# Splitting late weight loads and bias foldings, and reordering two steps beside causal attention, in a fused cross-attention and transformer block

## The chip, the cores and the metric

The kernel runs on one core of one Trainium2 chip. The metric is the device time of one execution in microseconds (us); lower is better. The kernel before took 955.61 us, the median of three runs that lay between 954.59 and 956.64.

## The reference

Two layers are computed for 16 batches of 256 tokens with 256 features; both use 16 heads of width 16, everything in float32.

```python
# layer 0: cross attention with RMS norms and a mask over the context (all true here)
Q = rmsnorm(x, g_q) @ Wq;  K, V = rmsnorm(ctx, g_c) @ (Wk, Wv)
x = rmsnorm(x + softmax(Q K^T * hd**-0.5, masked) V @ Wo, g_out)
# layer 1: a block with causal self attention, cross attention, and an MLP of 1024
h = ln(x);  q, k = rope(h @ sa_wq + b), rope(h @ sa_wk + b);  v = h @ sa_wv + b
x = x + causal_attention(q, k, v) @ sa_wo + sa_bo
h = ln(x);  q = rope(h @ ca_wq + b);  k, v = rope(y @ ca_wk + b), y @ ca_wv + b
x = x + attention(q, k, v) @ ca_wo + ca_bo
x = x + gelu(ln(x) @ fc1_w + fc1_b) @ fc2_w + fc2_b
```

The gains and biases of the layer norms are not applied to the activations. The kernel folds them into the weights ("gain": each row of the weight is multiplied) and into the biases ("bias": the norm's bias times the weight is added to the projection's bias).

## The kernel before, in words

There are 48 attentions: three for each batch, of type 0 (cross attention of the first layer), 1 (causal self attention) and 2 (cross attention of the second layer). `ORDER` (line 31) is a string of 48 digits that says which type comes at each place `i`; the batch is the count of that digit so far. The whole order is written out by hand in one schedule (line 878 on): a loop over `i`, and in it a loop over the blocks `n` of scores of attention `i`, four for types 0 and 2 and three for the causal type 1. Each engine executes its instructions in the order in which the schedule issues them. After the 48 attentions comes an MLP over pairs of batches, which takes the last quarter of the time.

At block `n` the schedule issues, always in this order: the scores of block `n` (`scores`, line 475: matmuls of line 488 into two PSUM tiles `S`, then two exponentials of ScalarE at line 499, then for causal blocks the masking selects of GpSimd at line 506), the product of probabilities and values of block `n-1` (`value`, line 517: matmuls of line 527 into the single PSUM tile `A`), and then the pieces of neighbouring attentions:

- `n = 0`: `end` of attention `i-1` (VectorE copies `A` to SBUF, line 544; SP sends it to DRAM and fetches the sums of the softmax and the outputs back turned, lines 552 and 557), `divide` of `i-2` (line 578), statistics of the norms of `i+2`, and `q` of `i+1`.
- `n = 1`: `invert` of `i-1` (VectorE takes the reciprocal of the sums at line 564, for type 0 after a clamp at line 563; SP sends it to DRAM at line 566 and fetches it back broadcast at line 572), then `k` of `i+1`.
- the block before the last: `v` of `i+1` (line 468 or 460); the last block: the output projection of `i-2` (`project`, line 584 or 587) and the turn of the normed rows of `i+2` (`turn`, transposes at line 267).

For types 1 and 2, `q` and `k` go through `rotated` (line 390): ScalarE adds the bias out of PSUM (line 395), VectorE shuffles a copy (line 399) and multiplies by the cosine and sine tables (line 403). `q` then adds the two (line 419) and writes two masked copies, one for even and one for odd heads, into `qm` (lines 420 and 424, or 422); `k` adds into `kT` (line 447). For type 0, `k` is only a copy by ScalarE (line 449) and `q` two VectorE operations (line 414).

Which engine makes the second masked copy is decided by the attention that runs meanwhile:

```python
        att(i + 1).q(shared=a.causal)
...
            if shared:
                nc.scalar.activation(self.qm[:, :, 1, :], a, AF.Copy, scale=parity[1])
```

Only types 1 and 2 get this far in `q`. In `ORDER` a causal attention is followed by type 2 five times (i = 21, 28, 38, 40, 42) and by type 0 eleven times, so line 422 runs five times.

Batches are loaded when `att(i+3)` is of type 0: four DMAs of 256 KB (lines 94, 95, 99, 101) at the start of attention `i`. All of these, the hops through DRAM and the later weights are issued on SP's one queue, in order. The later weights are loaded at fixed places: `ca` (768 KB) at i = 3, `cao` (256 KB) and `fc1` (1 MB) at i = 4, `fc2` (1 MB) at i = 6, each at block n = 2 (lines 1000 to 1008).

The biases are folded by `fold_bias` (line 166): matmuls with the norm's bias as the stationary operand, a copy by ScalarE (line 180) and a hop to DRAM; `fold_back` (line 185) fetches the result back as columns, element by element, into `cols`. The cross attention and `fc1` share one folding (bias at i = 6, n = 3; back at i = 8, n = 2; the adds of `fold_ca_fc1` on VectorE, lines 201 to 203, at i = 8, n = 3, after the gain of `ca`, line 223). The gain of `fc1` is two GpSimd operations at i = 10 and 12, and `combine` (line 629) issues one GpSimd operation at a time at n = 1 of the non-causal attentions from i = 14 on.

Of the kernel before, what the change touches and what calls it, by code (L numbers as in the profile page):

```python
# [8 lines left out]
F32 = mybir.dt.float32  # L9
U8 = mybir.dt.uint8  # L10
I32 = mybir.dt.int32
AF = mybir.ActivationFunctionType
ALU = mybir.AluOpType
AX = mybir.AxisListType

P = 128
B, S, D = 16, 256, 256
H, HD = 16, 16
FF = 1024
NC = S // P  # L20
KC = D // P
# [7 lines left out]
N_ATT = 3 * B  # L29
# [16 lines left out]
def xattn_kernel(  # L46
# [21 lines left out]
    nc = tc.nc  # L68

    const = ctx.enter_context(tc.tile_pool(name="const", bufs=1))  # L70
    small = ctx.enter_context(tc.tile_pool(name="small", bufs=4))
    work = tc.alloc_tile_pool(name="work", bufs=2)

    def ctile(shape, name, dtype=F32):
        return const.tile(shape, dtype, tag=name, name=name)
# [31 lines left out]
    def load_w(t, aps, eng):  # L107
        at = 0
        for a in aps:
            m = a.shape[1]  # L110
            eng.dma_start(out=t[:, :, at : at + m], in_=a.rearrange("(k p) n -> p k n", p=P))
            at += m


    vec = ctile([P, NVEC + 2], "vec")
# [7 lines left out]
    sa_sb = ctile([P, KC, 3 * D], "sa")  # L123
    sao_sb = ctile([P, KC, D], "sao")
    ca_sb = ctile([P, KC, 3 * D], "ca")
    cao_sb = ctile([P, KC, D], "cao")
    fc1_sb = ctile([P, KC, FF], "fc1")
    fc2_sb = ctile([P, FF // P, D], "fc2")
# [7 lines left out]
    parity = [vec[:, NVEC + i : NVEC + i + 1] for i in range(2)]  # L136
# [6 lines left out]
    dram = ctx.enter_context(tc.tile_pool(name="dram", bufs=2, space=bass.MemoryType.DRAM))  # L143
# [19 lines left out]
    qk_bias = ctile([P, 4, KC], "qk_bias")  # L163
    fb1 = ctile([P, FF // P], "fb1")

    def fold_bias(sets):

        ps = dense_ps()
        w = len(sets) * D
        for n, items in enumerate(sets):  # L170
            for k in range(KC):
                for j, (t, at, vcol) in enumerate(items):
                    nc.tensor.matmul(
                        ps[32 * j : 32 * j + 32, n * D : (n + 1) * D],
                        lhsT=vec[:, vcol + k : vcol + k + 1].to_broadcast([P, 32]),
                        rhs=t[:, k, at : at + D],
                        start=(k == 0), stop=(k == KC - 1), skip_group_check=True,
                    )
        sb = work.tile([P, 2 * D], F32, tag="a", name="fold")
        nc.scalar.copy(sb[:, :w], ps[:, :w])  # L180
        hop = dram.tile([4, w], F32, tag=f"fold{len(sets)}", name="fold_hop", bufs=1)
        nc.sync.dma_start(out=hop, in_=sb[0:P:32, :w])
        return hop

    def fold_back(hop):

        w = hop.shape[1]
        cols = ctile([P, 4, w // D, KC], f"cols{w // D}")
        nc.sync.dma_start(
            out=cols.rearrange("p j n t -> p (j n t)"),  # L190
            in_=hop.rearrange("j (m p) -> p (j m)", p=P),
        )
        return cols
# [1 line left out]
    qk_cols = vec[:, V_QK : V_QK + 8].rearrange("p (n t) -> p n t", t=KC)  # L195

    def fold_sa(cols):
        nc.vector.tensor_tensor(qk_bias[:, 0:2], cols[:, 0:2, 0], qk_cols[:, 0:2], ALU.add)

    def fold_ca_fc1(cols):  # L200
        nc.vector.tensor_tensor(qk_bias[:, 2], cols[:, 0, 0], qk_cols[:, 2], ALU.add)
        nc.vector.tensor_copy(qk_bias[:, 3], qk_cols[:, 3])
        nc.vector.tensor_tensor(
            fb1.rearrange("p (j t) -> p j t", t=KC), cols[:, :, 1],
            vec[:, V_FC1B : V_FC1B + FF // P].rearrange("p (j t) -> p j t", t=KC), ALU.add,
        )

# [13 lines left out]
    def fold_gain(w, cols, vcol, chunks=range(KC), eng=nc.vector):  # L221
        for k in chunks:
            eng.tensor_scalar(
                w[:, k, cols], w[:, k, cols], vec[:, vcol + k : vcol + k + 1], None, ALU.mult
            )
# [82 lines left out]
    class Att:  # L308
# [96 lines left out]
                )  # L405
            return a, u

        def q(self, shared=False):
            ps = by_feature(self.hT, self.w, 0)
            self.qm = work.tile([P, KC, 2, S], F32, tag="qm", name="qm", bufs=2)  # L410
            if self.layer == 0:
                rq = self.rq.unsqueeze(1).to_broadcast([P, KC, S])
                for i in range(2):
                    nc.vector.scalar_tensor_tensor(
                        self.qm[:, :, i, :], ps, parity[i], rq, ALU.mult, ALU.mult
                    )
                return
            a, u = self.rotated(ps, 0)
            nc.vector.tensor_tensor(a, a, u, ALU.add)
            nc.vector.tensor_scalar(self.qm[:, :, 0, :], a, parity[0], None, ALU.mult)  # L420
            if shared:
                nc.scalar.activation(self.qm[:, :, 1, :], a, AF.Copy, scale=parity[1])
            else:
                nc.vector.tensor_scalar(self.qm[:, :, 1, :], a, parity[1], None, ALU.mult)

        def first_qk(self):

# [171 lines left out]
    def att(i):  # L599
        if 0 <= i < N_ATT:  # L600
            return atts.setdefault(i, Att(i))
        return None

    def do(i, *names):
        a = att(i)
        for name in names:
            if a is not None:
                getattr(a, name)()
# [269 lines left out]
    with tc.manual_schedule():  # L878
# [25 lines left out]
        for j in range(N_ATT):  # L904
            slot = next(i for i in range(max(j - 1, 0), N_ATT + 1) if (ORDER + [0])[i] != 1)
            kept.setdefault(slot, []).append(j)
        for i in range(N_ATT):
            a, last = att(i), att(i - 1)
            ahead = att(i + 3)
# [10 lines left out]
            for n in range(len(a.blocks)):  # L920
# [8 lines left out]
                if n == 0:  # L929
                    if i == 0:  # L930
                        a.v()
                        do(1, "spread")
                    late = finishing and i + 2 < N_ATT and att(i + 2).layer == 0
                    if not follows and not late and (finishing or not a.causal):
                        do(i + 2, "stats")
                    do(i - 1, "end")
                    if late:
                        do(i + 2, "stats")
                    do(i - 3, "finish")
                    if follows:  # L940
                        do(i + 2, "stats")
                    if not finishing:
                        do(i + 2, "norm")
                    if i == N_ATT - 3:
                        mlps[0].stats()
                    if i == N_ATT - 2:
                        mlps[0].norm()
                    do(i - 2, "divide")
                    if i == N_ATT - 1:
                        mlps[0].turn(nc.vector.tensor_copy)  # L950
                        mlps[0].keep()
                    if i + 1 < N_ATT:

                        att(i + 1).q(shared=a.causal)
                elif n == 1:
                    if last is not None:
                        last.invert(lambda: do(i + 2, "send"))
                    else:
                        do(i + 2, "send")
                    do(i + 2, "receive")  # L960
                    do(i + 1, "k")
                    if finishing:
                        do(i + 2, "norm")
                    for j in kept.get(i, ()):
                        att(j).keep()
                    if i == N_ATT - 1:
                        do(i - 2, "project")
                        mlps[1].norm()
# [23 lines left out]
                        out=rope_sb, in_=rope.rearrange("(c p) t d -> p c t d", p=P)  # L992
                    )
                if i == 1 and n == 3:
                    sa_hop = fold_bias([[(sa_sb, 0, V_B1), (sa_sb, D, V_B1)] * 2])
                if i == 2 and n == 2:
                    sa_cols = fold_back(sa_hop)
                if i == 2 and n == 3:
                    fold_gain(sa_sb, slice(0, 3 * D), V_G1)
                if i == 3 and n == 2:  # L1000
                    load_w(ca_sb, ca, nc.sync)
                if i == 3 and n == 3:
                    fold_sa(sa_cols)
                if i == 4 and n == 2:
                    load_w(cao_sb, [ca_o], nc.sync)
                    load_w(fc1_sb, [fc1], nc.sync)
                if i == 6 and n == 2:
                    load_w(fc2_sb, [fc2], nc.sync)
                if i == 6 and n == 3:
                    ca_hop = fold_bias(  # L1010
                        [[(ca_sb, 0, V_B2)] * 4, [(fc1_sb, j * D, V_B3) for j in range(4)]]
                    )
                if i == 8 and n == 2:
                    ca_cols = fold_back(ca_hop)
                if i == 8 and n == 3:
                    fold_gain(ca_sb, slice(0, D), V_G2)
                    fold_ca_fc1(ca_cols)
                if i in (10, 12) and n == 1:
                    fold_gain(fc1_sb, slice(0, FF), V_G3, [i // 12], nc.gpsimd)
                if n == 1 and i > 12 and not a.causal:  # L1020
                    next(combined, None)

        last = att(N_ATT - 1)
# [486 lines left out]
```

## Time and profile before

| quantity | value |
|---|---|
| median of three runs | 955.61 us (954.59 to 956.64) |
| the profiled execution, its own time | 953.12 us |
| its span from first to last instruction | 951.4 us |
| TensorE matmul (PE) busy | 936.0 us, 98% of the span |
| weight loads (PEld) busy | 551.9 us, 58% |
| VectorE (DVE) busy | 663.8 us, 70% |
| ScalarE (ACT) busy | 548.8 us, 58% |
| GpSimd (POOL) busy | 306.9 us, 32% |
| moved by DMA | 83.07 MB, mean 87 GB/s |
| exponentials of ACT, line 499 | 352 of 1022 or 1111 ns |
| granted TensorE clock | full throughout |

An attention is told apart in the trace by its first score matmul (line 488). From one such matmul to the next, an attention takes between 13.29 us (most causal ones) and 16.22 us (a non-causal one that turns rows and follows a causal one), so a few tenths of a microsecond of waiting show as a longer stretch of its kind. "Busy" of PE includes matmuls whose ends are modelled; the lengths of the stretches tell more than the share.

### The profile page before, as it was taken

The page shows a single profiled execution, that of the slowest core. Times are in us where ns is not written, and L with a number is a line of the kernel's source. Part 1 is how long each engine was busy: PE and PEld are TensorE (multiplying, and loading weights), DVE is VectorE, ACT ScalarE, POOL GpSimd, SP SyncE. Part 2 cuts the span into 40 slices and gives each one's busy share as a digit, 9 for nine tenths or more (in the row PEclk, how much of TensorE's full clock was granted, in tenths as well). Part 3 has the DMA queues.
Part 4 walks back from the last instruction along what each step waited for, and adds up shares of the span by engine and source line. Part 5 has one row for each costly group of instructions (what it writes and reads, how often), then busy time and mean ns, then how long its engine had stood idle before and what let it go on. Part 6 is the DMA issues. An engine that isn't in the chain of part 4 may idle for free.

```text
span 951.4 us, 29306 instructions
## 1 busy us (share of the span) xinstructions
PE 936.0 (98%) x12390; PEld 551.9 (58%) x12390; DVE 663.8 (70%) x1434; ACT 548.8 (58%) x777; POOL 306.9 (32%) x503
## 2 busy tenths in 40 slices
PE   8999999999999999999999999999999999999997
PEld 4444454445454455454454445455444799999997
DVE  4448666877777777867866767887877576676663
ACT  4666555766666665756656666666666634444440
POOL 3214353434344364243343423443233021222200
PEclk9999999999999999999999999999999999999999
DMA  9444353323232323222334222222222100000001
GB/s 302 135 118 155 123 170 82 119 77 116 86 121 71 113 83 127 64 88 92 100 124 127 80 82 68 72 70 71 71 69 72 57 23 20 13 14 24 23 24 47
DMA packets 99005, 83.07 MB, mean 87 GB/s; under 512 B 22570, under 2 KB 98350, under 8 KB 98866
## 3 DMA queue, kind: packets, MB, share of 16 engines
q1 hardware_dynamic: 98178, 80.58, 26.7%
q8 instruction: 99, 1.62, 0.7%
q10 hardware_dynamic: 688, 0.54, 0.2%
q14 instruction: 40, 0.33, 0.1%
HBM read 50.92 MB, written 30.17 MB: 85 GB/s over the span
## 4 chain that ended last, share of the span: by engine, by line
PE 88%; DVE 5%; DMA 3%; ACT 2%; issue 1%; SPq 1%; POOL 0%; ACTq 0%; DVEq 0%
PE S L488 18%; PE A L527 17%; PE d L287 15%; PE d L300 14%; PE upX L692 6%; PE A L790 5%; PE upZ L692 3%; PE downZ L790 3%; PE d L267 2%; PE d L790 2%; PE d L692 1%; ACT pt L499 1%; DVE u L399 1%; DVE u L403 1%; ACT a L395 1%; DVE a L403 1%
## 5 line engine op out<-in xcount | busy, mean ns | idle before, releaser
L499 ACT ACTIVATE pt<-S 128x1024 f32<-128x1024 f32 x224 | 217.2, 1022 | 111.4 <-PE S L488 111.4
L488 PE MATMUL S<-qm,kT 32*128 32x512 f32 (+1 forms) x1536 | 206.3, 600 | 2.9 <-DVE kT L447 2.9
L527 PE MATMUL A<-pt,va 128*32 128x256 f32 (+1 forms) x3072 | 188.7, 367 | 1.0 <-DVE av L544 1.0
L527 PEld LDWEIGHTS A<-pt,va 128*32 128x32 f32 x3072 | 80.1, 109 | 154.4 <-issue 104.1
L499 ACT ACTIVATE pt<-S,sy 128x1024 f32<-128x1024 f32 x128 | 135.6, 1111 | 46.5 <-PE S L488 45.9
L506 POOL TENSOR_SCALAR_AFFINE_SELECT pt<-pt 128x512 f32<-128x512 f32 x128 | 86.4, 693 | 70.0 <-ACT pt L499 69.7
L488 PEld LDWEIGHTS S<-qm,kT 32*128 32x128 f32 x1536 | 63.8, 183 | 71.5 <-issue 42.8
L231 POOL TENSOR_SCALAR r_ln<-bmv 128x2 f32<-128x2 f32 x48 | 14.1, 293 | 223.8 <-DVE bmv L250 222.7
L276 POOL TENSOR_TENSOR cur<-cur,bias 128x512 f32<-128x512 f32 x48 | 66.6, 1393 | 56.7 <-DVE xn L256 56.7
L395 ACT ACTIVATE a<-d,qk_bias 128x256 f32<-128x256 f32 x128 | 53.6, 471 | 47.8 <-PE d L287 37.5
L287 PE MATMUL d<-hT,sa 128*32 128x256 f32 x1024 | 61.1, 379 | 0.0
L587 DVE TENSOR_TENSOR cur<-d,cur 128x512 f32<-128x512 f32 x32 | 22.0, 688 | 50.3 <-PE d L300 50.2
L256 DVE TENSOR_SCALAR xn<-cur,bmv,r_ln 128x256 f32<-128x256 f32 x96 | 53.5, 606 | 0.8 <-POOL r_ln L232 0.3
L403 DVE TENSOR_TENSOR u<-u,turn 128x512 f32<-128x512 f32 x64 | 51.8, 810 | 0.0
L544 DVE COPY av<-A 128x512 f32<-128x512 f32 x47 | 32.4, 689 | 27.3 <-PE A L527 26.3
L403 DVE TENSOR_TENSOR a<-a,turn 128x512 f32<-128x512 f32 x64 | 47.8, 747 | 2.2
L399 DVE STREAM_SHUFFLE u<-a 128x512 f32<-128x512 f32 x64 | 47.6, 744 | 0.0
L730 ACT ACTIVATE g<-g,fb 128x256 f32<-128x256 f32 x96 | 41.0, 499 | 11.1 <-DVE g L719 11.1
L287 PEld LDWEIGHTS d<-hT,sa 128*32 128x32 f32 x1024 | 33.3, 110 | 22.0
L231 POOL TENSOR_SCALAR r_o<-ms_o 128x2 f32<-128x2 f32 x16 | 3.9, 243 | 123.0 <-DVE sq L239 113.4
L578 DVE TENSOR_TENSOR oT<-oT,inv 128x512 f32<-128x512 f32 x48 | 43.0, 896 | 0.5 <-DMA inv<-inv_hop 0.5
L785 DVE TENSOR_TENSOR g<-g,g 128x512 f32<-128x512 f32 x64 | 40.9, 681 | 0.0
(154 smaller groups left out, 1566.8 us busy)
## 6 DMA issues: line engine op xcount, KB each, us to landing
hop<-av SPq DMA_DIRECT2D x96, 256.0 KB
oT<-hop SPq DMA_DIRECT2D x96, 128.0 KB
inv<-inv_hop SPq DMA_DIRECT2D x96, 128.0 KB
xT<-in_xt SPq DMA_DIRECT2D x16, 256.0 KB
cur<-in_x SPq DMA_DIRECT2D x16, 256.0 KB
yT<-in_yt SPq DMA_DIRECT2D x16, 256.0 KB
y<-in_y SPq DMA_DIRECT2D x16, 256.0 KB
out<-res SPq DMA_DIRECT2D x15, 256.0 KB
```

Source lines behind the costliest of these rows:

```text
L276: nc.gpsimd.tensor_tensor(t, t, bias_sb[:, row : row + D].unsqueeze(1).to_broadcast([P, NC, D]), ALU.add)
L287: nc.tensor.matmul(ps[j : j + 32, t * S : (t + 1) * S], lhsT=w[:, k, at + t * P + j : at + t * P + j + 32], rhs=src[:, k, :], start=(k == ...
L300: nc.tensor.matmul(ps[j : j + 32, c * D : (c + 1) * D], lhsT=src[:, k, c * P + j : c * P + j + 32], rhs=w[:, k, at : at + D], start=(k == ...
L395: nc.scalar.activation(a[:, t], ps[:, t], AF.Identity, bias=bias[:, t : t + 1])
L399: nc.vector.stream_shuffle(u.rearrange("p t s -> p (t s)"), a.rearrange("p t s -> p (t s)"), SWAP)
L403: nc.vector.tensor_tensor(t, t, table.unsqueeze(1).to_broadcast([P, KC, S]), ALU.mult)
L488: nc.tensor.matmul(ps[:, j, 2 * m * u : 2 * m * (u + 1)] .rearrange("p (i s) -> p i s", i=2), lhsT=self.kT[r, t, kc * P : (kc + 1) * P], r ...
L499: nc.scalar.activation(pt[:, :, :w], ps[:, :, :w], AF.Exp, scale=scale)
L506: nc.gpsimd.affine_select(out=diag, in_=diag, compare_op=ALU.is_ge, fill=0.0, base=0, pattern=[[0, 2], [0, 2], [1, P]], channel_multiplier=-1,
L527: nc.tensor.matmul(self.av[32 * r : 32 * r + 32, i, q0:S], lhsT=self.va[:, kc, 8 * t + 2 * r + i, :], rhs=pts[r // 2][:, r % 2, i * m : (i ...
L692: nc.tensor.matmul(banks[c // 2][:, (c % 2) * S : (c % 2 + 1) * S], lhsT=a[:, c * P : (c + 1) * P], rhs=b, start=(first and c % 2 == 0), s ...
L790: nc.tensor.matmul(ps[:, c, :], lhsT=a[f // 2][:, f % 2, c * P : (c + 1) * P], rhs=b[:, f, :], start=(first and c == 0 and f == 0), stop=True,
```

## The change

Four edits are made together.

1. Later weights: the four loads are cut into twelve pieces of 256 KB (three of `ca`, one `cao`, four column pieces of `fc1`, four row pieces of `fc2`). One piece is issued on SP at n = 1 and one at n = 2 of each attention from i = 4 on for which no batch is loaded (`att(i+3)` is not of type 0): i = 4, 6, 8, 9, 10 and 12.
2. Foldings: the folding shared by the cross attention and `fc1` becomes two. That of the cross attention keeps its matmuls at i = 6, n = 3 and its return at i = 8, n = 2, and its gain and adds now follow at once, still at n = 2. That of `fc1` has its matmuls at i = 11, n = 3, its return and its add both at i = 14, n = 2. The gain of `fc1` moves to i = 14 and 15, and `combine` starts after i = 15.
3. Both masked copies of `q` are always made on VectorE.
4. In causal attentions `k` of `i+1` is issued ahead of `invert` of `i-1`.

```diff
-    def fold_bias(sets):
+    def fold_bias(items):
...
-        hop = dram.tile([4, w], F32, tag=f"fold{len(sets)}", name="fold_hop", bufs=1)
-        nc.sync.dma_start(out=hop, in_=sb[0:P:32, :w])
+        hop = dram.tile([4, D], F32, tag="fold", name="fold_hop")
+        nc.sync.dma_start(out=hop, in_=sb[0:P:32, :D])
         return hop
...
-        cols = ctile([P, 4, w // D, KC], f"cols{w // D}")
+        cols = small.tile([P, 4, KC], F32, tag="cols", name="cols")
...
-    def fold_ca_fc1(cols):
-        nc.vector.tensor_tensor(qk_bias[:, 2], cols[:, 0, 0], qk_cols[:, 2], ALU.add)
+    def fold_ca(cols):
+        nc.vector.tensor_tensor(qk_bias[:, 2], cols[:, 0], qk_cols[:, 2], ALU.add)
         nc.vector.tensor_copy(qk_bias[:, 3], qk_cols[:, 3])
+
+    def fold_fc1(cols):
         nc.vector.tensor_tensor(
-            fb1.rearrange("p (j t) -> p j t", t=KC), cols[:, :, 1],
+            fb1.rearrange("p (j t) -> p j t", t=KC), cols,
...
-            nc.vector.tensor_scalar(self.qm[:, :, 0, :], a, parity[0], None, ALU.mult)
-            if shared:
-                nc.scalar.activation(self.qm[:, :, 1, :], a, AF.Copy, scale=parity[1])
-            else:
-                nc.vector.tensor_scalar(self.qm[:, :, 1, :], a, parity[1], None, ALU.mult)
+            for i in range(2):
+                nc.vector.tensor_scalar(self.qm[:, :, i, :], a, parity[i], None, ALU.mult)
...
+        pieces = [(ca_sb[:, :, j * D : (j + 1) * D], [ca[j]], nc.sync) for j in range(3)]
+        pieces.append((cao_sb, [ca_o], nc.sync))
+        for j in range(4):
+            cols = slice(j * D, (j + 1) * D)
+            pieces.append((fc1_sb[:, :, cols], [fc1[:, cols]], nc.sync))
+        for j in range(4):
+            pieces.append((fc2_sb[:, 2 * j : 2 * j + 2], [fc2[j * D : (j + 1) * D]], nc.sync))
...
                 elif n == 1:
+
+                    if a.causal:
+                        do(i + 1, "k")
                     if last is not None:
                         last.invert(lambda: do(i + 2, "send"))
                     else:
                         do(i + 2, "send")
                     do(i + 2, "receive")
-                    do(i + 1, "k")
+                    if not a.causal:
+                        do(i + 1, "k")
...
-                if i == 3 and n == 2:
-                    load_w(ca_sb, ca, nc.sync)
                 if i == 3 and n == 3:
                     fold_sa(sa_cols)
-                if i == 4 and n == 2:
-                    load_w(cao_sb, [ca_o], nc.sync)
-                    load_w(fc1_sb, [fc1], nc.sync)
-                if i == 6 and n == 2:
-                    load_w(fc2_sb, [fc2], nc.sync)
+                if i > 3 and n in (1, 2) and ahead is not None and ahead.layer > 0:
+                    for piece in pieces[:1]:
+                        load_w(*piece)
+                    del pieces[:1]
                 if i == 6 and n == 3:
-                    ca_hop = fold_bias(
-                        [[(ca_sb, 0, V_B2)] * 4, [(fc1_sb, j * D, V_B3) for j in range(4)]]
-                    )
+                    ca_hop = fold_bias([(ca_sb, 0, V_B2)] * 4)
                 if i == 8 and n == 2:
                     ca_cols = fold_back(ca_hop)
-                if i == 8 and n == 3:
                     fold_gain(ca_sb, slice(0, D), V_G2)
-                    fold_ca_fc1(ca_cols)
-                if i in (10, 12) and n == 1:
-                    fold_gain(fc1_sb, slice(0, FF), V_G3, [i // 12], nc.gpsimd)
-                if n == 1 and i > 12 and not a.causal:
+                    fold_ca(ca_cols)
+                if i == 11 and n == 3:
+                    fc1_hop = fold_bias([(fc1_sb, j * D, V_B3) for j in range(4)])
+                if i == 14 and n == 2:
+                    fold_fc1(fold_back(fc1_hop))
+                if i in (14, 15) and n == 1:
+                    fold_gain(fc1_sb, slice(0, FF), V_G3, [i - 14], nc.gpsimd)
+                if n == 1 and i > 15 and not a.causal:
                     next(combined, None)
```

More of the change, by code (lines that the diff above doesn't have):

```diff
@@ L164, in xattn_kernel @@
     fb1 = ctile([P, FF // P], "fb1")
-    def fold_bias(sets):
+    def fold_bias(items):
         ps = dense_ps()
[L169 to L177, printed above, removed]
-                    )
+        for k in range(KC):
+            for j, (t, at, vcol) in enumerate(items):
+                nc.tensor.matmul(
+                    ps[32 * j : 32 * j + 32, :D],
+                    lhsT=vec[:, vcol + k : vcol + k + 1].to_broadcast([P, 32]),
+                    rhs=t[:, k, at : at + D],
+                    start=(k == 0), stop=(k == KC - 1), skip_group_check=True,
+                )
         sb = work.tile([P, 2 * D], F32, tag="a", name="fold")
-        nc.scalar.copy(sb[:, :w], ps[:, :w])
-        hop = dram.tile([4, w], F32, tag=f"fold{len(sets)}", name="fold_hop", bufs=1)
-        nc.sync.dma_start(out=hop, in_=sb[0:P:32, :w])
+        nc.scalar.copy(sb[:, :D], ps[:, :D])
+        hop = dram.tile([4, D], F32, tag="fold", name="fold_hop")
+        nc.sync.dma_start(out=hop, in_=sb[0:P:32, :D])
         return hop
     def fold_back(hop):
-        w = hop.shape[1]
-        cols = ctile([P, 4, w // D, KC], f"cols{w // D}")
+        cols = small.tile([P, 4, KC], F32, tag="cols", name="cols")
         nc.sync.dma_start(
-            out=cols.rearrange("p j n t -> p (j n t)"),
+            out=cols.rearrange("p j t -> p (j t)"),
             in_=hop.rearrange("j (m p) -> p (j m)", p=P),
@@ L197, in fold_sa @@
     def fold_sa(cols):
-        nc.vector.tensor_tensor(qk_bias[:, 0:2], cols[:, 0:2, 0], qk_cols[:, 0:2], ALU.add)
-    def fold_ca_fc1(cols):
-        nc.vector.tensor_tensor(qk_bias[:, 2], cols[:, 0, 0], qk_cols[:, 2], ALU.add)
+        nc.vector.tensor_tensor(qk_bias[:, 0:2], cols[:, 0:2], qk_cols[:, 0:2], ALU.add)
+    def fold_ca(cols):
+        nc.vector.tensor_tensor(qk_bias[:, 2], cols[:, 0], qk_cols[:, 2], ALU.add)
         nc.vector.tensor_copy(qk_bias[:, 3], qk_cols[:, 3])
+    def fold_fc1(cols):
         nc.vector.tensor_tensor(
-            fb1.rearrange("p (j t) -> p j t", t=KC), cols[:, :, 1],
+            fb1.rearrange("p (j t) -> p j t", t=KC), cols,
             vec[:, V_FC1B : V_FC1B + FF // P].rearrange("p (j t) -> p j t", t=KC), ALU.add,
@@ L406, in rotated, with q @@
             return a, u
-        def q(self, shared=False):
+        def q(self):
             ps = by_feature(self.hT, self.w, 0)
@@ L951, in xattn_kernel @@
                         mlps[0].keep()
-                    if i + 1 < N_ATT:
-                        att(i + 1).q(shared=a.causal)
+                    do(i + 1, "q")
                 elif n == 1:
+                    if a.causal:
+                        do(i + 1, "k")
                     if last is not None:
@@ L994, in xattn_kernel @@
                 if i == 1 and n == 3:
-                    sa_hop = fold_bias([[(sa_sb, 0, V_B1), (sa_sb, D, V_B1)] * 2])
+                    sa_hop = fold_bias([(sa_sb, 0, V_B1), (sa_sb, D, V_B1)] * 2)
                 if i == 2 and n == 2:
@@ L999, in xattn_kernel @@
                     fold_gain(sa_sb, slice(0, 3 * D), V_G1)
-                if i == 3 and n == 2:
-                    load_w(ca_sb, ca, nc.sync)
                 if i == 3 and n == 3:
                     fold_sa(sa_cols)
-                if i == 4 and n == 2:
-                    load_w(cao_sb, [ca_o], nc.sync)
-                    load_w(fc1_sb, [fc1], nc.sync)
-                if i == 6 and n == 2:
-                    load_w(fc2_sb, [fc2], nc.sync)
+                if i > 3 and n in (1, 2) and ahead is not None and ahead.layer > 0:
+                    for piece in pieces[:1]:
+                        load_w(*piece)
+                    del pieces[:1]
                 if i == 6 and n == 3:
-                    ca_hop = fold_bias(
-                        [[(ca_sb, 0, V_B2)] * 4, [(fc1_sb, j * D, V_B3) for j in range(4)]]
-                    )
+                    ca_hop = fold_bias([(ca_sb, 0, V_B2)] * 4)
                 if i == 8 and n == 2:
                     ca_cols = fold_back(ca_hop)
-                if i == 8 and n == 3:
                     fold_gain(ca_sb, slice(0, D), V_G2)
-                    fold_ca_fc1(ca_cols)
-                if i in (10, 12) and n == 1:
-                    fold_gain(fc1_sb, slice(0, FF), V_G3, [i // 12], nc.gpsimd)
-                if n == 1 and i > 12 and not a.causal:
+                    fold_ca(ca_cols)
[6 more added lines that the diff above has]
+                if n == 1 and i > 15 and not a.causal:
                     next(combined, None)
```

## The prediction

> **What bounds the kernel now.** I read the page first, then stretches from one attention's first score matmul to the next's, then the list of waits, then the chain inside one stretch.
>
> ```profile
> PE 936.0 (98%) x12390; PEld 551.9 (58%) x12390; DVE 663.8 (70%) x1434; ACT 548.8 (58%) x777; POOL 306.9 (32%) x503
> ```
>
> PE is busy nearly throughout, so at most the difference from its own pace can be won. Busy time does not show that difference. Stretches of one kind do. The window view gives length, busy PE, PEld, DVE, ACT, POOL, clock, DMA share and GB/s:
>
> ```profile
> core 0: us, PE busy (x) PEld busy (x) DVE busy (x) ACT busy (x) POOL busy (x), PEclk, DMA share, GB/s
> 301.71:315.00 13.29, 13.29 (x217) 7.10 (x213) 7.59 (x15) 6.88 (x8) 6.40 (x12) 1.00 0.28 89
> 331.22:346.12 14.90, 14.32 (x214) 7.41 (x213) 11.09 (x23) 9.49 (x14) 7.58 (x12) 1.00 0.40 131
> 88.08:103.70 15.62, 13.37 (x216) 7.08 (x213) 7.76 (x21) 6.88 (x8) 7.86 (x14) 1.00 0.66 217
> 121.06:135.16 14.10, 13.37 (x217) 7.08 (x213) 7.06 (x18) 7.47 (x9) 7.96 (x14) 1.00 0.63 197
> 150.78:165.13 14.35, 13.36 (x217) 7.62 (x213) 9.92 (x27) 6.88 (x8) 7.82 (x14) 1.00 0.23 48
> ```
>
> The first row is a causal attention (i = 19) at PE's pace, 13.29 us for the same matmuls; eight of sixteen keep it. The second (i = 21, ahead of a type 2) takes 14.90, and so do i = 28, 38, 40 and 42, within 0.01. The others are i = 5, 7 and 9: 2.33, 0.81 and 1.06 us over. Non-causal stretches after the start show no such excess. The waits name the causes (total, times, longest):
>
> ```profile
> ACT qm L422 <- DVE a L419: 14.6, 5, 2.9
> PE S L488 <- DVE kT L447: 2.9, 5, 0.6
> PE d L267 <- DVE xn L256: 3.0, 2, 2.3
> PE A L527 <- DVE av L544: 1.0, 1, 1.0
> DVE sums L563 <- DMA sums<-hop: 26.3, 9, 7.5
> ```
>
> The chain inside i = 21 (start, length, what) shows how the first two make 1.61 us:
>
> ```profile
> 338.13 0.70 DVE a L419
> ...
> 338.92 0.72 ACT qm L422
> 339.64 1.82 ACT pt L499 x2
> 341.47 0.74 ACT a L395 x2
> ...
> 344.96 1.02 DVE kT L447
> ...
> 346.12 1.09 PE S L488 x5
> ```
>
> ScalarE stands 2.9 us at the second mask, waiting for VectorE. The exponentials of block 1, whose scores ended near 336.1, start only at 339.6. So the score tiles are freed late and PE's block 2 takes 1.97 instead of 1.07 us (0.90 lost). Behind the exponentials the bias of k comes late, hence `kT`; PE waits with the next attention's scores from 345.5 (0.65 lost, with a few hundredths between).
>
> [...] stretches of equal work differ by 1.61 us while PE looks 96% busy in the longer. [...] So `cols` starts behind what SP issued before; its packets of 4 bytes begin near 150.2 in the trace, after those of the hop issued ahead of it. [...] beside GpSimd's gain of `fc1` at i = 12, line 419 took 1.40 us for its usual 0.69, but the hold is shorter than the whole GpSimd operation (4.03 us there).
>
> **Part by part.** All is measured against the profiled execution: 953.12 us, of which 951.4 is span and 1.7 lies around it. The median of runs, 955.61, stands 2.5 above; I subtract the same microseconds from it.
>
> *Both masks on VectorE, and k ahead of the reciprocal.* Five ScalarE operations of 0.72 us go, five VectorE ones of 0.49 us (line 420's row) come; type 0 never reaches this line. The moved `k` changes a queue only in the same five places: for the other eleven `k` is PE and ScalarE work, `invert` VectorE and SP work. At i = 21, recomputed: exponentials of block 1 from 336.2 to 338.1; k's matmuls end at 338.7, the bias by 339.7; VectorE's masks end at 339.85, then shuffle 0.75, two products 0.69 and 0.61, add 0.69: `kT` at 342.7. PE, not stopped in block 2, wants it at 344.6: 1.9 us of cover, about 0.9 if GpSimd's selects slow VectorE. Both stalls go: 5 x 1.61 = **8.05 us gained**. VectorE's busy time in the stretch becomes 11.1 + 0.5 = 11.6 of 13.3 us; it fits.
>
> What is late instead is the reciprocal, at 343.3 for 339.8. Line 566 holds SP until then; the two fetches of line 572 go out 1.5 us after it, take 1.2 to issue, and their last packets come 1.7 us later, as before (342.5 to 344.2): 347.8. Behind them on SP is only the hop of block 1's output, needed an attention later. `divide` (line 578) comes at 349.43 less 1.6 saved = 347.9. It meets the landing, so I take zero. The output is projected three blocks on.
>
> *Twelve pieces.* At i = 5, 1.25 MB of weights and 1 MB of batch run together (217 GB/s). The hop of line 545 lands late and VectorE stands 7.5 us at the sums, with the normed rows for line 267 behind it. At i = 7 it is `fc2` with a batch. Afterwards these two carry a batch alone, as i = 31 and 33 do: their reciprocals came at 9.1 and 7.8 us from the start, and i = 9, without load, works with 10.3. The stalls go: 2.33 + 0.81 = **3.14 gained**. The pieces themselves (0.5 us of SP each) lie in stretches at 23 to 40% DMA share, in front of no urgent transfer except `cols`.
>
> *Folding of the cross attention.* Before, at i = 8:
>
> ```profile
> 153.95 0.36 DVE L201 TENSOR_TENSOR qk_bias<-cols,vec 128x2 f32<-128x2 f32 x1 [0.87 <-DMA cols<-fold_hop]
> ```
>
> Gain, wait and adds held VectorE from 152.47 to 154.82, and line 544 freed `A` 1.06 us late. So the slack there is 2.35 - 1.06 = 1.29 us. **That 1.06 goes.** Now the gain fits into VectorE's gap (147.9 to 150.9), and the wait stands in front of line 584, which wants 150.92. SP issues two pieces first, so `cols` goes out at 149.9 instead of 148.8. Ahead of it some 900 packets of 1 KB drain, at 320 per us (the rate while a batch loads), by 152; then 1024 elements follow, half as many, in 1 us: landing 153, adds 0.4. Line 584 is 2.5 us late, PE 2.5 - 1.29 = **1.2 lost**. Bounds: 0 if it lands by 151.8, 3.6 if some packets straggle as before (the last 129 came 1.5 us after the rest).
>
> *Folding of fc1.* The same wait at i = 14, with nothing between issue and use. The hop ahead is issued by 240.0; `cols` then lands near 243.4, or 244.4 because the GpSimd gain (3.46 us for a combine step of 1.31) slows q and k of i = 15. The add takes 0.60. From landing to a free `A` VectorE still has 0.6 + 0.6 (line 587) + 1.8 (four squares) + 0.7 (line 544) = 3.7; PE wants it at 246.69: 244.4 + 3.7 - 246.7 = **1.4 lost**, bounds 0 and 3.3. PE's matmuls stay 32, but two sets cost 0.98 each where one cost 1.84: **0.1 lost**. The later combine steps meet covered GpSimd time: zero, at most 0.5.
>
> Sum: 8.05 + 3.14 + 1.06 - 1.2 - 1.4 - 0.1 = 9.5. Own time 943.6, span 941.9; median 955.61 - 9.5 = **946.1 us**.
>
> **Rivals.** *A, the foldings wait hardly or long.* Same direction: both lower bounds give 12.1 gained, 943.5; both upper ones 5.2, 950.4. For: the packets that straggled; against: half the elements.
>
> *B, half the causal gain.* If GpSimd's selects slow VectorE until `kT` misses its time, the 0.65 stays: 9.5 - 3.3 = 6.2 gained, 949.4. For: lines 403 took 0.9 to 1.1 there; against: 0.9 us of cover remain.
>
> *C, slower.* The late reciprocal. Past `divide`, VectorE next wants the shuffle of q at 351.42 (1.3 us later), and the `kT` of i = 23 is ready 1.1 us ahead of use. So a landing over 2.4 us late stops PE at each of five places; from 2.4 + 9.5/5 = 4.3 us late, that is 352.1 instead of 347.8, the gain is gone, and at 5.5 late the time is 955.6 + 5 x 3.1 - 9.5 = 961.6. The chain from reciprocal to landing took 4.7 us at i = 21 beside a batch load, so nothing speaks for twice that.
>
> *D, nothing happens,* because PE's pace hides it: 955.6. The stretches of 13.29 with the same matmuls speak against it.
>
> **Chances.** My forecast with A 0.78, B 0.12, C 0.05, D 0.05. A measurement can tell about 0.2% (1.9 us). Faster 0.90, same 0.05, slower 0.05. Range: from 942.3 (best bounds, and a microsecond of spread between runs) to 951.0 (both foldings at their worst, with a little more).
>
> **What would show it.** Right: i = 21, 28, 38, 40 and 42 at 13.3 us, no wait of ScalarE on line 419, i = 5 and 7 at 13.3, and VectorE waiting for `cols` 1.5 to 3 us at i = 8 and more at i = 14, with a PE wait on line 544 in i = 9 and 15. Wrong: stretches above 14 in the five places, a wait at line 578 for the inverse, or a wait at `cols` above 5 us.

## The result and the profile after

The changed kernel took 948.96 us, the median of seven runs (946.45 to 951.07), against 955.61 for seven runs of the kernel before (951.58 to 957.32). The ratio is 0.9939, with a 95% interval of 0.9917 to 0.9961: faster by 0.4 to 0.8%. The profiled execution took 948.64 us with a span of 946.9, so 4.5 us of span went, where 9.5 were forecast.

First the stretches of the changed kernel that answer to those shown before, in the window view (same columns; i = 21, 5, 7, 9 and, new here, 15):

```profile
core 0: us, PE busy (x) PEld busy (x) DVE busy (x) ACT busy (x) POOL busy (x), PEclk, DMA share, GB/s
335.09:348.38 13.29, 13.29 (x214) 7.09 (x213) 11.49 (x22) 8.56 (x12) 8.31 (x12) 1.00 0.39 122
89.41:103.50 14.09, 13.36 (x216) 7.07 (x212) 8.62 (x21) 6.88 (x8) 7.87 (x14) 1.00 0.62 190
120.00:133.28 13.28, 13.28 (x216) 7.09 (x212) 8.16 (x21) 7.26 (x9) 7.96 (x14) 1.00 0.59 187
148.91:166.94 18.03, 15.51 (x217) 7.58 (x213) 9.32 (x24) 6.88 (x8) 7.77 (x14) 0.91 0.29 83
244.63:260.89 16.26, 15.26 (x225) 7.38 (x224) 12.66 (x28) 10.49 (x14) 8.67 (x9) 1.00 0.22 58
```

The causal attention ahead of a type 2 is at PE's pace, 13.29 us; so are the other four. i = 7 is at pace too, and 0.8 us stay in i = 5. Against that stands i = 9, 4.74 us over its pace where it was 1.06 before, and its clock column, 0.91, is the only one under 1.00. i = 15 is 1.07 over.

The list of waits of the changed kernel (total, times, longest) has lost ScalarE's wait for the mask and PE's for `kT`. Among its new lines are these two:

```profile
DVE qk_bias L198 <- DMA cols<-fold_hop: 6.3, 1, 6.3
DVE fb L202 <- DMA cols<-fold_hop: 5.6, 1, 5.6
```

The whole difference of the two spans, stretch by stretch:

| where | before | after | difference |
|---|---|---|---|
| up to the first scores, and i = 0 | 26.67 | 27.99 | +1.32 |
| i = 21, 28, 38, 40, 42 | 5 x 14.90 | 5 x 13.29 | -8.05 |
| i = 5 | 15.62 | 14.09 | -1.53 |
| i = 7 | 14.10 | 13.29 | -0.81 |
| i = 9 | 14.34 | 18.03 | +3.69 |
| i = 15 | 15.19 | 16.26 | +1.07 |
| i = 6 and 11 (one folding with two sets, or two) | 33.14 | 33.27 | +0.13 |
| i = 22 and the rest | | | +0.08 |
| i = 47 and the MLP | 225.91 | 225.53 | -0.38 |

The sum is -4.5. The first row is the initial load: over the profiled executions here it lies between 26.7 and 28.3, for the changed kernel and its variants alone between 26.8 and 28.3, so its 1.3 us are not put down to the change.

What happened in i = 9 stands in the timeline of VectorE and of PE (start, length, engine, line, what, and in brackets the wait ahead of it):

```profile
152.79 0.16 DVE L198 TENSOR_TENSOR qk_bias<-cols,vec 128x2 f32<-128x2 f32 x1 [6.26 <-DMA cols<-fold_hop]
152.87 0.16 DVE L199 COPY qk_bias<-vec 128x2 f32<-128x2 f32 x1
152.94 0.68 DVE L580 TENSOR_TENSOR s<-d,cur 128x512 f32<-128x512 f32 x1
...
155.56 0.67 DVE L540 COPY av<-A 128x512 f32<-128x512 f32 x1
```

```profile
152.71 1.15 PE L484 MATMUL S<-qm,kT 32*128 32x256 f32 x16
156.38 1.45 PE L523 MATMUL A<-pt,va 128*32 128x256 f32 x8 [2.52 <-POOL pt L502]
```

VectorE frees `A` at 156.2 (line 540, line 544 of the kernel before), and PE, standing from 153.9, goes on at 156.4. That is 2.52 us of the 4.74. The other 2.2 (2.1 or 2.15 in the expectations below, which reckon with 13.36 us of busy PE instead of 13.29) come after PE has started again, and the window view of these parts shows how:

```profile
148.91:152.70 3.79, 3.79 (x60) 1.77 (x56) 0.00 (x0) 1.94 (x2) 0.00 (x0) 1.00 0.57 142
152.70:156.40 3.70, 1.18 (x22) 0.78 (x19) 3.47 (x13) 1.94 (x2) 1.67 (x4) 1.00 0.00 0
156.40:159.80 3.40, 3.40 (x32) 1.37 (x36) 2.92 (x5) 0.00 (x0) 3.23 (x6) 0.53 0.23 77
```

In the third row PE is busy all the time, at a mean clock of 0.53 (the stretch at 0.50 lasts 3.41 us and begins at 156.57, a little behind the start of this row). It does 32 matmuls in 3.40 us, where the experiment e8_filler, below, does 54 at full clock.

### The profile page after: what moved, and what is told of

Read it like the earlier page. It is cut to its first block, busy times and chain, and to the rows that moved or that the text cites. A ratio compares the mean times of both kernels' runs of the same rounds, so it can differ in the third digit from the quotient of the medians.

```text
span 946.9 us, 29342 instructions
## 1 busy us (share of the span) xinstructions
PE 934.5 (99%) x12390; PEld 551.1 (58%) x12390; DVE 664.8 (70%) x1439; ACT 547.0 (58%) x773; POOL 310.6 (33%) x503
## 4 chain that ended last, share of the span: by engine, by line
PE 91%; DMA 4%; DVE 2%; SPq 1%; issue 1%; POOL 0%; ACT 0%; ACTq 0%; DVEq 0%
PE S L484 18%; PE A L523 17%; PE d L286 16%; PE d L299 16%; PE upX L688 6%; PE A L786 5%; PE downZ L786 3%; PE upZ L688 3%; PE d L266 2%; PE d L786 2%; PE d L688 1%; DMA hop<-av 1%; DMA cols<-fold_hop 1%; PE d L664 1%; PE downX L786 1%
## 5 line engine op out<-in xcount | busy, mean ns | idle before, releaser
L484 PE MATMUL S<-qm,kT 32*128 32x512 f32 (+1 forms) x1536 | 201.8, 600 | 0.0
L502 POOL TENSOR_SCALAR_AFFINE_SELECT pt<-pt 128x512 f32<-128x512 f32 x128 | 88.8, 709 | 62.5 <-ACT pt L495 62.2
L230 POOL TENSOR_SCALAR r_ln<-bmv 128x2 f32<-128x2 f32 x48 | 14.1, 295 | 214.7 <-DVE bmv L249 213.5
L402 DVE TENSOR_TENSOR u<-u,turn 128x512 f32<-128x512 f32 x64 | 49.7, 777 | 0.0
```

The lines of the kernel that those rows point to most:

```text
L402: nc.vector.tensor_tensor(t, t, table.unsqueeze(1).to_broadcast([P, KC, S]), ALU.mult)
L484: nc.tensor.matmul(ps[:, j, 2 * m * u : 2 * m * (u + 1)] .rearrange("p (i s) -> p i s", i=2), lhsT=self.kT[r, t, kc * P : (kc + 1) * P], r ...
L502: nc.gpsimd.affine_select(out=diag, in_=diag, compare_op=ALU.is_ge, fill=0.0, base=0, pattern=[[0, 2], [0, 2], [1, P]], channel_multiplier=-1,
```

## The experiments

Two theories stood for the gain: that ScalarE's wait is the one root of the causal stalls, or that each edit removes its own part. For the loss, the late columns of the folding were the theory, with GpSimd's queue or the clock behind the second half.

**e1_masks: both masks alone.**

```diff
-                        att(i + 1).q(shared=a.causal)
+                        att(i + 1).q()
```

> The kernel before with one edit: both masked copies of q on VectorE. Theory 1 (ScalarE's wait for the second mask is the only root in the five causal attentions; the late bias of k is its consequence): i = 21, 28, 38, 40 and 42 fall from 14.90 to 13.29-13.3 us, all 8.05 us, because kT would then be ready near 343.3 where PE wants it at 344.6. Theory 2 (each of the two edits removes one of the two stalls): only the 0.90 us in the second block goes and the 0.65 us at kT stays, 13.9-14.0 us each. Everything else as before: i = 5, 7, 9 at 15.6, 14.1, 14.3.

Measured: i = 38, 40 and 42 fall to 13.36 us, i = 21 and 28 to 14.05. Of 8.05 us, 6.3 come with this edit. Neither theory is quite right. The one execution took 948.01 us, as long as the changed kernel: by the stretches, the other edits together bring nothing, since what they gain is less than what the foldings lose. The timeline of VectorE in i = 21 shows what is left:

```profile
341.23 0.74 DVE L420 TENSOR_SCALAR qm<-a,vec 128x512 f32<-128x512 f32 x1
341.90 0.85 DVE L424 TENSOR_SCALAR qm<-a,vec 128x512 f32<-128x512 f32 x1
342.67 0.20 DVE L563 TENSOR_SCALAR sums<-sums 128x32 f32<-128x32 f32 x1
342.91 0.35 DVE L564 RECIPROCAL sums<-sums 128x32 f32<-128x32 f32 x1
...
344.58 1.12 DVE L403 TENSOR_TENSOR u<-u,turn 128x512 f32<-128x512 f32 x1
345.74 1.01 DVE L447 TENSOR_TENSOR kT<-a,u 128x512 f32<-128x512 f32 x1
```

The two masks take 0.74 and 0.85 us where line 420 took 0.49 before. In the profile after, which has both masks on VectorE too, GpSimd's selects start 6.1 us into i = 21 (9.4 before) and run from 341.2 to 344.7, beside the last steps of `q` (341.3 to 345.0, the masks 1.51 us together). (Line 447 is no news: it took 1.02 us in i = 21 before, too.) The masks are done late, the reciprocal with its clamp puts the work for `k` another 0.5 us later, and `kT` ends at 346.75, when PE has been standing since 346.19. In the changed kernel, where `k` comes first, its second product (line 403 here) takes 0.68 instead of 1.12 us (346.31 to 346.99; the next select starts at 346.75). GpSimd's part in the longer operations is my reading of the overlap in the profile after and was not tried by itself.

**e2_kfirst: k ahead of the reciprocal alone.** The diff is that of the change at `n == 1`, with the mask left on ScalarE.

> The kernel before with one edit: k ahead of the reciprocal in causal attentions, the second mask still on ScalarE. Theory 1: the five stretches stay at 14.8-14.9 us, since the bias of k on ScalarE is late in either order; the reciprocal moves to near 346.6 of i = 21's clock, 6 to 7 us later, the inverse lands 1 to 2 us after divide wants it, and the following attention still keeps its length. Theory 2: the 0.65 us goes, 14.2-14.3 each. A rival to both: the late inverse shows, and the attentions after the five grow by over 0.5 us.

Measured: the five stay at 14.89 to 14.90 us. ScalarE waits 14.6 us at the mask as before, and the late reciprocal shows:

```profile
DVE oT L578 <- DMA inv<-inv_hop: 5.1, 5, 1.9
```

VectorE waits up to 1.9 us for the inverse, yet i = 22, 29, 39, 41 and 43 keep their length. The edit is worth nothing alone, and 1.7 us (8.05 - 6.3) on top of the masks. So the first theory holds for the root: without the mask's wait gone, the order of `k` and the reciprocal does not matter.

In the same run i = 5 and 6, where its code is that of the kernel before, take 17.52 and 19.73 us (15.62 and 17.36 in the profile before; 16.56 and 18.49 in e1_masks), while i = 7 is at 13.29 in both. The load of weights beside a batch costs between 3.1 and 6.6 us in i = 5 to 7, different from one execution to the next.

**e3_whole: the changed kernel without pieces.**

```diff
+                if i == 3 and n == 2:
+                    load_w(ca_sb, ca, nc.sync)
-                if i > 3 and n in (1, 2) and ahead is not None and ahead.layer > 0:
-                    for piece in pieces[:1]:
-                        load_w(*piece)
-                    del pieces[:1]
+                if i == 4 and n == 2:
+                    load_w(cao_sb, [ca_o], nc.sync)
+                    load_w(fc1_sb, [fc1], nc.sync)
+                if i == 6 and n == 2:
+                    load_w(fc2_sb, [fc2], nc.sync)
```

> The changed kernel with the later weights loaded whole and at the old places (no pieces). If the pieces removed the stalls of i = 5 and 7, these return: 15.6 and 14.1 us for 14.09 and 13.29. If the two pieces issued ahead of the return of the folding at i = 8 are what made it land late, i = 9 shortens from 18.0 to about 16.5 (VectorE waits about 4.8 instead of 6.3 us); if the wait is the transfer's own time, i = 9 stays within 0.4 of 18.0.

Measured in the window view (i = 5, 6, a part of 6, 7 and 9):

```profile
89.49:105.00 15.51, 13.36 (x216) 7.07 (x212) 7.75 (x21) 6.89 (x8) 7.88 (x14) 1.00 0.67 220
105.00:123.13 18.13, 18.13 (x258) 8.49 (x257) 14.58 (x36) 11.22 (x14) 6.22 (x10) 0.91 0.28 85
105.33:108.74 3.41, 3.41 (x36) 1.38 (x32) 1.62 (x6) 2.21 (x3) 0.95 (x2) 0.50 0.29 89
123.13:137.23 14.10, 13.37 (x217) 7.08 (x213) 7.50 (x20) 7.25 (x9) 7.71 (x14) 1.00 0.63 210
152.86:168.34 15.48, 13.96 (x216) 7.24 (x213) 8.83 (x24) 6.89 (x8) 7.78 (x14) 1.00 0.19 49
```

The stalls of i = 5 and 7 return, and i = 6 runs 3.41 us at half clock after PE's wait in i = 5. i = 9 takes 15.48 instead of 18.03, and VectorE waits 4.8 instead of 6.3 us. So in this pair of executions the pieces gain 3.9 us in i = 5 to 7 and give back 2.6 in i = 9, where two of them stand ahead of the columns: without these, SP has issued the columns 14.0 instead of 14.8 us after the start of i = 8, with some 420 instead of 740 packets of 1 KB left ahead of them. It is one execution; the four with pieces and early adds waited 6.3 to 7.2 us. i = 15 came out at 15.40; no piece is near it, and with 15.3 to 16.3 in all runs that keep its wait it varies by itself.

**e4_adds_late: the same DMAs, the adds issued later.**

```diff
                     fold_gain(ca_sb, slice(0, D), V_G2)
+                if i == 9 and n == 2:
                     fold_ca(ca_cols)
...
-                    fold_fc1(fold_back(fc1_hop))
+                    fc1_cols = fold_back(fc1_hop)
+                if i == 15 and n == 2:
+                    fold_fc1(fc1_cols)
```

> The changed kernel with the two adds of the foldings issued later than the return of their columns: those of the cross attention at i = 9, n = 2 and that of fc1 at i = 15, n = 2; all loads and DMAs as in the changed kernel. If VectorE's wait for the columns is the root of the stalls in i = 9 and 15, i = 9 falls from 18.03 to 13.3 and i = 15 from 16.26 to 15.2 us, 5.8 us less in all. If GpSimd in i = 9 is late for a reason of its own (the square root of project, the DMA traffic), 2.1 us of it stay: 15.4.

Measured, i = 9 and i = 15:

```profile
147.83:161.12 13.29, 13.29 (x217) 7.10 (x213) 8.69 (x22) 6.89 (x8) 7.88 (x14) 1.00 0.32 88
238.81:254.00 15.19, 15.19 (x225) 7.08 (x224) 12.29 (x28) 10.51 (x14) 8.77 (x9) 1.00 0.25 67
```

Both stand at PE's pace, VectorE waits nowhere for `cols`, and the run took 941.88 us. VectorE's wait is the root of everything lost in i = 9 and 15.

**e6_ro_behind: GpSimd's root behind the selects.** In `project`, for attention i = 6 alone (called batch 6 below), only the squares are summed, and `inv_sqrt` follows in `finish`.

> The changed kernel, but for batch 6 alone GpSimd's two operations of the inverse root after project (lines 230 and 231) are issued one block later, behind the masking selects of i = 9's first block. If 2.15 of the 4.74 us in i = 9 come from the selects standing behind these two in GpSimd's queue, i = 9 falls from 18.03 to 15.9 us, with PE waiting only for line 540. If PE waits for the tile A alone and GpSimd is merely named last, i = 9 stays within 0.3 of 18.0.

Measured: i = 9 took 19.02 us, so neither figure came, and my theory that GpSimd's queue makes all of the second half fell. The waits of PE say that GpSimd no longer ends the wait, and that the wait stays:

```profile
PE A L523 <- DVE av L540: 4.1, 1, 4.1
```

VectorE waited 7.2 us for the columns in this run, 0.9 more than in the profile after (SP issued them 1.6 us later), and the half clock followed again:

```profile
158.03:161.44 3.41, 3.33 (x32) 1.84 (x36) 1.85 (x3) 0.00 (x0) 3.26 (x7) 0.50 0.25 82
```

Of the 5.73 us over its pace, PE stood for 4.05. The other 1.68 are near the 1.7 us (3.41 / 2) that a rate in step with the clock of 0.50 would cost, an estimate. With the selects out of the way this part is still there; the 0.5 us that the profile after has on top of it is not.

**after_again and e5_from_six.** The changed kernel once more, beside a kernel with late adds in which the twelve pieces start at i = 6.

> The changed kernel itself, timed beside e5_from_six on one chip: 949 us, ratio to the kernel before 0.993 to 0.995. i = 9 near 18.0 and i = 15 at 15.4 to 16.3 us again if the late columns are a fixed cost of the order; if they are a matter of chance in the transfer, i = 9 comes out over 1 us away from 18.0.

> The changed kernel with the adds of both foldings issued late (as in e4_adds_late) and, besides, no piece at i = 4: the twelve start at i = 6 and end at i = 13. If the two pieces of i = 4, which SP issues only just ahead of the batch of i = 5, are the cause of the 0.8 us left there, i = 5 is 13.3 instead of 14.1 us and i = 6 stays 16.5; if the batch alone makes it, i = 5 stays near 14.1. i = 9 and 15 stay at 13.3 and 15.2. Time: 955.6 - 8.05 (five causal) - 1.06 (i = 9) - 3.1 to 4.7 (i = 5 to 7) = 941.8 to 943.4, against the kernel before a ratio of 0.986 to 0.988.

after_again: 949.93 us, ratio 0.9929 (0.9905 to 0.9953). i = 9 took 19.89 us: VectorE waited 7.0 us, PE 3.4, and the clock was halved for 6.83 us instead of 3.41. The loss is thus 4.7 to 6.6 us, different from one execution to the next with the transfer and with the clock.

e5_from_six: i = 5 was 13.29 us as expected, but i = 6 took 21.60 and i = 7 15.29, and the gain was gone: 948.86 us where 941.8 to 943.4 were expected, ratio 0.9924 (0.9897 to 0.9950). The waits of PE name my mistake:

```profile
PE d L171 <- DMA ca<-in_ca_wq: 4.0, 1, 4.0
```

The folding at i = 6, n = 3 needs the first piece, issued at i = 6, n = 1 in the schedule. In SP's order it stands behind the hops. PE stood for 4.0 us, and then had a clock of 0.50 for 6.8 us.

**e7_one_early and e4_timed.** One piece at i = 4 and the rest from i = 6, against the kernel of e4_adds_late, both timed.

```diff
-                if i > 3 and n in (1, 2) and ahead is not None and ahead.layer > 0:
+                if (i > 5 and n in (1, 2) or i == 4 and n == 1) and ahead is not None and ahead.layer > 0:
```

> The kernel of e4_adds_late with one piece (the query weights of the cross attention) at i = 4 and the other eleven from i = 6 on. The folding at i = 6 finds its weights loaded, so the 5 us of e5_from_six do not return; with 256 KB less ahead of the batch of i = 5, i = 5 falls from 14.1 to 13.3-13.7. In all 0.3 to 0.8 us under e4_timed, too little to be told in the times; the stretches tell it. If even one piece ahead of the batch makes the stall, i = 5 stays at 14.1.

> The kernel of e4_adds_late once more, timed in rounds: 5.8 us in i = 9 and 15 gone from the changed kernel's 949 (more where its stall was longer), so 942 to 943.5 us; ratio to the kernel before 0.986 to 0.988. i = 9 at 13.3, i = 15 at 15.2, and i = 5 near 14.1 to 14.6.

e4_timed: 943.78 us, 0.3 above the expected range, ratio 0.9872 (0.9849 to 0.9894), i = 5 at 14.12. e7_one_early: 942.82 us, ratio 0.9866 (0.9843 to 0.9889), and i = 5 to 7 all at pace:

```profile
88.17:101.45 13.28, 13.28 (x216) 7.09 (x212) 8.00 (x21) 6.89 (x8) 7.92 (x14) 1.00 0.57 181
101.45:117.95 16.50, 16.50 (x258) 8.04 (x257) 14.45 (x35) 11.21 (x14) 6.20 (x10) 1.00 0.29 90
117.95:131.23 13.28, 13.28 (x216) 7.09 (x212) 8.16 (x21) 7.25 (x9) 7.97 (x14) 1.00 0.58 187
```

The times do not tell the two apart; both beat the changed kernel. With two pieces at i = 4, i = 5 took 14.1 to 14.6 us in five of six profiles. The two pieces leave SP at 88.9 and 89.9 in the profile after, the batch from 90.4: what the schedule places two blocks apart from a batch leaves side by side with it, since SP had waited on the hops (between 81.3 and 85.6 it issued nothing). The sixth profile, e8_filler, has i = 5 at pace and i = 7 at 14.10. So the one profile of e7_one_early fits its expectation, but that the second piece makes the stall of i = 5 is not shown.

**e8_filler: work for PE while it waits.** The changed kernel with

```diff
                 a.scores(n)
+                if i == 9 and n == 1:
+                    filler = dense_ps()
+                    for _ in range(3):
+                        nc.tensor.matmul(filler, lhsT=ident, rhs=turn_sb, start=True, stop=True)
```

> The changed kernel with three more matmuls (128 x 512, their result is read by nobody) on PE between the scores and the values of i = 9's second block, where PE stood still. They fill about 2.6 us. If half of the loss in i = 9 is the clock that drops after PE has stood still, no stretch at half clock follows and i = 9 takes 15.9 to 16.8 us, 2 us less, with more work. If the second half comes from GpSimd's queue, i = 9 stays at 18.0 or above.

Measured: VectorE waited 6.3 us as in the profile after, and i = 9 took 16.91 us, 1.1 less with 2.84 us of matmuls more:

```profile
149.12:166.03 16.91, 16.74 (x223) 8.89 (x219) 9.19 (x24) 6.88 (x8) 7.77 (x14) 1.00 0.26 70
```

The clock stays full, and what comes on top of the standing (or of the matmuls that fill it) falls from 2.2 to 0.8 us (16.91 - 13.29 - 2.84). So most of the second half of the loss, 1.4 of 2.2 us, went with the half clock. The result is 0.1 above my range: the 0.8 us lie inside the values' matmuls, where the second select of GpSimd is not done (PE's timeline names 0.17 of it so). So GpSimd's queue has a part in it, of which 0.17 us is shown.

## Why the prediction held, and where it did not

The time lies in the forecast range (942.3 to 951.0), 2.9 us above the forecast; the direction held, and the gains came where they were forecast. The price of the folding and the gain of the pieces were wrong in size, and two costs were not in the sum. In the pair of profiles 4.5 us went, less than half of the 9.5. That the medians differ by 6.7 fits the old loads of i = 5 to 7, which cost more in other executions of their code (4.4 us in e1_masks, 6.6 in e2_kfirst) than the 3.1 that I had counted; that part of the hit is luck.

- *Both masks, and k first: right to the hundredth.* 5 x 1.61 = 8.05 us, forecast and measured. But the cover of `kT` was 0.35 us at i = 21 (ready at 348.03, wanted at 348.38), not 1.9 or 0.9. I had priced the end of `q` at the old durations; beside GpSimd's selects the masks were done 1.2 us later than in my sum. That all 8.05 us came is thus a near thing: in e1_masks, 0.97 us later, `kT` cost 0.7 us. The two edits carry 6.3 and 1.7 us, a split that the prediction left open.
- *The late reciprocal (rival C): put at zero, and not always free.* In i = 22 VectorE stood at line 574 from 352.4 to 354.2, 1.8 us where I had zero, under the 2.4 that I had worked out as the point from which PE stops; i = 22 is 0.08 us longer. But "Behind them on SP is only the hop of block 1's output" fails at i = 29, which loads a batch: there the four loads stand behind the late fetches of the inverse and leave SP from 3.8 us after the start of i = 29, where they left from 1.2 us ahead of it in the profile before. The sums come back later, VectorE waits 1.7 to 3.2 us for them at line 560, and `k` of i = 30 stands behind. In the profile after this just fits (16.23 us). In six of the eight other profiles with both edits i = 29 is 0.2 to 1.5 us longer than the 16.22 before, most in e8_filler (waits of PE):

```profile
PE S L484 <- DVE kT L443: 1.5, 1, 1.5
```

- *Twelve pieces: 2.3 of 3.14 us.* Failed step: "Afterwards these two carry a batch alone". The pieces of i = 4 leave SP together with the batch of i = 5.
- *Folding of the cross attention: +3.69 us where I had +0.2 (1.2 lost less 1.06 gone).* Two terms failed. The landing: SP had issued `cols` 14.8 us after the start of i = 8, as forecast, and VectorE could use it at 19.5 instead of 17.8. By the packets in the trace, most of the 1 KB packets ahead had started by 17.2 (16.8 in my sum), the last elements came at 18.7, and another 0.8 us passed before the add, for which I had nothing. That made PE stand for 2.52 instead of 1.2 us. And a term that was not in the sum at all: after this standing the clock is halved for 3.41 us, and with GpSimd's second select that costs 2.2 us more. My upper bound of 3.6 held for the wait, not for what the wait costs. The figure of 1.5 to 3 us for VectorE's wait at i = 8 also contradicted my own sum, which leaves it free at 148.6 and has the columns at 153; the mark for being wrong, over 5 us, was passed. Rival A's bad end (5.2 us gained) is nearest to what the profile shows.
- *Folding of fc1: 1.07 us for 1.4.* The step held, with PE waiting 1.0 us at line 540 and no drop of the clock; over the five profiles that keep this wait it costs 0.15 to 1.1.
- *The rest.* Two sets of matmuls cost 0.13 us for 0.1.

The sum in its own terms: 8.05 + 2.34 - 3.69 - 1.07 - 0.13 = 5.5 us of forecast 9.5. The 4.5 of the spans is a microsecond less: the initial load of this execution took 1.3 us more, and 0.4 came back at the end.

## What to carry to other kernels

Price an add by the wait that stands in front of it in its engine's order: two tiny operations of 0.16 us cost PE up to 6.6 us, and moving them four blocks later, with every transfer as it was, gave all of it back (ratio 0.9872). Where TensorE stood for 2.15 us or more here, a clock of 0.50 followed in all of the cases listed below but one (2.25 us, none), for 3.41 or 6.83 us. It came on top of the standing, with 1.7 us in i = 9 of e6_ro_behind (3.41 us at 0.50) and 3.2 us in that of after_again (6.83 us; 19.89 - 13.29 - 3.36), and belongs into the price of such a wait. A place in a schedule is not a time on a DMA queue: the two pieces issued at n = 1 and 2 of i = 4 left SP at 88.9 and 89.9, behind hops that it had waited for until 85.6, and so beside the batch that leaves from 90.4. So ask of a step that is made late what else stands behind it on the queue, at each place where it occurs.

## What was new of the hardware

After PE had stood, its granted clock was in some places 0.50, for 3.41 us or twice that:

| kernel, place | PE stood, us | at a clock of 0.50 |
|---|---|---|
| after, i = 5 and 15; before, i = 9 | 0.7 to 1.0 | none |
| before, i = 5 | 2.25 | none |
| e3_whole, i = 5 | 2.15 | 3.41 us |
| after, i = 9 | 2.52 | 3.41 |
| e1_masks, i = 5 | 2.80 | 3.41 |
| after_again, i = 9 | 3.36 | 6.83 |
| e2_kfirst, i = 5 | 3.73 | 6.83 |
| e5_from_six, i = 6 | 4.03 | 6.83 |
| e6_ro_behind, i = 9 | 4.05 | 3.41 |

The length of the wait alone does not tell it: 2.25 us in the kernel before were followed by full clock, 2.15 us in e3_whole by 3.41 us at 0.50 (from 105.33, shown above), and 4.05 us in e6_ro_behind by half as long a stretch as 4.03 us in e5_from_six. What else decides was not shown. So a wait of about two microseconds cost 0.1 us beside itself in one run (2.33 us over the pace in i = 5) and 1.6 us in another: i = 6 behind it took 18.13 us in e3_whole, at 0.91 of full clock, and 16.50 in e7_one_early, at full clock.
